# One 8 MB store ahead of the middle loads, issued as two halves on two queues (pairwise products of 32 fields)

## The chip, the core and the metric

The kernel runs on one core of a Trainium2 chip. The metric is device time in microseconds (us) of one execution, the median over runs. The engines that matter here are TensorE (PE), VectorE (DVE), and the two engines that only issue transfers in this kernel: SyncE (SP) and ScalarE (ACT). Each of the two has a queue of its own into the core's 16 DMA engines: in the profile SP's is q1 and ACT's is q10.

## The reference

For each of 4096 rows with 32 fields of 64 numbers, all fields are multiplied by one 64x64 matrix, and every pair of fields i < j gives one product, element by element. That makes 496 pairs, and an output of 4096 x 496 x 64 float32, 520 MB, from an input of 33.6 MB.

```python
vid = jnp.einsum('bfd,de->bfe', x, W)              # x: (4096, 32, 64), W: (64, 64)
idx_i, idx_j = jnp.triu_indices(32, k=1)           # 496 pairs
return x[:, idx_i, :] * vid[:, idx_j, :]           # (4096, 496, 64)
```

## The kernel before

**Tiles.** The batch is cut into 16 tiles (`NT`). A tile has 32 units, one for each field; a unit is 128 partitions x 128 float32 (two halves of the batch times 64 numbers on the partitions, 128 rows along a partition), 512 bytes on each partition. TensorE writes `vid` for one tile into PSUM in two halves of 16 fields. DVE multiplies: a unit of `x` in SBUF times a unit of `vid` gives a unit of the output, 496 of them to a tile.

**One buffer.** All of SBUF is one tensor, `mem`, of 445 units. The input lies in units 0 to 255, eight tiles at a time; `GROUPS` says so: group 0 is tiles 0 to 7, group 1 is tiles 8 to 15. The output is a stream of 7936 units, cut by the table `SLOTS` into 74 slots of 51 to 128 units. Each slot has a home in `mem`: as the input tiles of a group are used up, slots take their place. A slot is stored by one DMA when its last unit is made (`store`, L258). Slot 36, for example, is 128 units at home 304, so units 304 to 431, 8 MB in all, 64 KB to a partition.

**The middle loads.** When tile 8 begins (`t in begins[1:]`, L272), `load(1)` issues three loads for group 1: units 154 to 255 (6.7 MB, it holds tiles 8 and later), 26 to 153 (8.4 MB) and 0 to 25 (1.7 MB). Each waits (`after`, L201) until the stores that read its units have landed and DVE is done with the input there. In issue order the transfers are numbered `moved0`, `moved1` and so on; before the change `moved39`, `moved40` and `moved41` are the stores of slots 34, 35 and 36, and `moved42`, `moved43` and `moved44` are the three middle loads. The first store behind the loads, slot 37, also waits for the second of them (`hold[-2]`, L264).

**Queues.** Loads and the stores of slots 0 to 45 are issued by SP, in program order; those of slot 46 (`SECOND`) and later by ACT. An engine that issues stands still at an instruction until its semaphores are reached, so what stands behind it in its queue waits too. `Queue.waits` (L135) leaves out a wait that follows from an earlier one. `STRETCHES = [37]` marks slot 37 as the first slot behind the middle loads; so slot 36 is the last store ahead of them.

At the end SP waits for every transfer (L313).

Of the kernel before, what the change touches and what calls it, by code (L numbers as in the profile page):

```python
# [24 lines left out]
STRETCHES = [37]  # L25
# [17 lines left out]
SECOND = 46  # L43
# [128 lines left out]
def pairwise_bilinear_kernel(nc, x0, x, out):  # L172
# [8 lines left out]
    mem = ctx.enter_context(nc.sbuf_tensor([P, UNITS, C], F32))  # L181
# [8 lines left out]
    sp, act, dve = (Queue(engine, behind) for engine in (nc.sync, nc.scalar, nc.vector))  # L190
    moved = []
    worked = []

    def transfer(out_, in_, units, reads, needs, queue=sp):
        sem = nc.alloc_semaphore(f"moved{len(moved)}")
        queue.issue(lambda: queue.engine.dma_start(out=out_, in_=in_), needs).then_inc(sem, 16)  # L196
        queue.note(sem, 16)
        moved.append((units, reads, sem))
        return sem

    def after(units):  # L201

        needs = [(s, 16) for u, reads, s in moved if reads and overlap(u, units)]
        last = max((n for spans, n in worked if any(overlap(units, s) for s in spans)), default=0)
        return needs + [(made, last)] * (last > 0)
# [52 lines left out]
    def store(slot, last):  # L258
        nonlocal hold
        begin, end = STARTS[slot : slot + 2]  # L260
        home = SLOTS[slot][1]
        units = (home, home + end - begin)
        needs = [(made, last)]
        if hold:  # L264
            needs.append((hold[-2], 16))
            hold = []
        rows = out[BLOCKS[slot] : BLOCKS[slot + 1], :].rearrange("(p u) c -> p u c", p=P)
        transfer(rows[:, : end - begin, :], mem[:, units[0] : units[1], :], units, True, needs, act if slot >= SECOND else sp)


    for t in range(NT):
        if t in begins[1:]:  # L272
            hold = load(begins.index(t))
            for late in held:
                store(*late)
            held = []
        xs = (place_of(t, F), place_of(t, F) + F)
        blocks = list(products(by_block(), t * NP))
        for k, (at, n, nest, i, j) in enumerate(blocks):
            slot = bisect_right(STARTS, at) - 1  # L280
            begin, end = STARTS[slot], STARTS[slot + 1]
            home = SLOTS[slot][1]
            units = (home + at - begin, home + at - begin + n)
# [11 lines left out]
            needs = [(there, 2 * t + 2 - high), *after(units)]  # L295
# [9 lines left out]
            if at == end:  # L305
                late = (slot, counts[made])
                group = sum(behind <= slot for behind in STRETCHES)
                if t < begins[group]:
                    held.append(late)
                else:  # L310
                    store(*late)
# [65 lines left out]
```

## Time and profile before

| what | value |
|---|---|
| time, three runs | 1283.78, 1283.85, 1284.95 us; median 1283.85 us |
| span of the profiled execution | 1282.6 us (first to last instruction; what lies around it is no part of it) |
| bytes moved | 553.7 MB, 520.1 MB of them written to HBM |
| DVE busy | 1079.9 us, 84% of the span |
| PE busy | 179.4 us, 14% |
| last store before the middle loads (slot 36) | issued at 603.93 us, landed 38.0 us later |
| middle loads issued | from 622.22 us |

The page has the profiled execution's span alone; the median of the runs stands 1.25 us above it. Rows of a timeline begin with a time in us from the start of the span. In a table of stretches the last three columns are the granted TensorE clock, the share of time in which the 16 DMA engines were busy and the rate in GB/s. A packet is put down whole to the stretch in which it starts, so a short stretch can show a share over 1.

### The profile page before, as it was taken

Reading aid. Unit: us, or ns where it says so; the run is one execution under the profiler, and the core shown is the slowest. Engines: PE = TensorE matmul, PEld = TensorE weight load, DVE = VectorE, ACT = ScalarE, POOL = GpSimd, SP = SyncE. Lnnn points to the kernel's source line nnn. Section 1 sums busy time; section 2 is a strip of 40 time slices with the busy share of each in tenths; the row PEclk is TensorE's granted clock in tenths of the full one; section 3 lists DMA queues with packets and bytes.
Section 4 is the critical chain, followed back from the end, with each engine's and each line's share of the span. In section 5 each row is a group of like instructions: output and inputs, shape, how many; then the busy total and the mean of one; then the engine's idle time right before and its main releaser. Section 6 shows DMA issues by size and latency. Waiting matters only on the chain. (4 is left out here: it accounts for less than half of the span.)

```text
span 1282.6 us, 1255 instructions
## 1 busy us (share of the span) xinstructions
PE 179.4 (14%) x256; PEld 70.2 (5%) x256; DVE 1079.9 (84%) x273; POOL 0.2 (0%) x4
## 2 busy tenths in 40 slices
PE   2011120301111030300020111103020020201100
PEld 1000000100000010100010000001010010100000
DVE  6589989988897989998027989989988899899980
POOL 0000000000000000000000000000000000000000
PEclk8566565756656565655565655656556575656555
DMA  9999999999999999999999999999999999999999
GB/s 404 423 435 435 438 433 433 439 435 425 435 444 429 425 437 442 428 425 446 416 426 437 426 433 436 438 434 434 439 431 442 421 437 435 427 446 429 434 425 409
DMA packets 11810, 553.70 MB, mean 432 GB/s; under 512 B 1312, under 2 KB 1312, under 8 KB 1312
## 3 DMA queue, kind: packets, MB, share of 16 engines
q1 hardware_dynamic: 7776, 340.30, 61.5%
q10 hardware_dynamic: 4032, 213.39, 38.4%
q14 instruction: 2, 0.02, 0.0%
HBM read 33.59 MB, written 520.09 MB: 432 GB/s over the span
## 5 line engine op out<-in xcount | busy, mean ns | idle before, releaser
L299 DVE TENSOR_TENSOR mem<-mem,vid 128x1024 f32<-128x1024 f32 (+11 forms) x270 | 1079.3, 4065 | 161.2 <-DMA out_dram<-mem 114.5
L319 PE MATMUL vid<-mem,w 128*128 x256 | 179.4, 866 | 1016.1 <-PEq L317 1016.1
L319 PEld LDWEIGHTS vid<-mem,w 128*128 128x128 f32 x256 | 70.2, 288 | 1124.4 <-issue 1124.4
L230 DVE COPY w<-mem 64x64 f32<-64x64 f32 x2 | 0.4, 191 | 5.1 <-DMA mem<-in_r_x_dram 5.0
L227 DVE MEMSET w<- 128x128 f32 x1 | 0.2, 165 | 0.8 <-PEq L344 0.8
L344 POOL MEMSET const-bfloat16-1.0<- 128x1 bf16 x1 | 0.1, 101 | 0.0
L344 POOL MEMSET const-uint8-127<- 128x1 uint8 x1 | 0.1, 101 | 0.0
L344 POOL MEMSET const-float32-0.0<- 128x1 f32 x1 | 0.1, 98 | 0.2 <-issue 0.2
L344 POOL MEMSET const-float32-1.0<- 128x1 f32 x1 | 0.1, 98 | 0.0
## 6 DMA issues: line engine op xcount, KB each, us to landing
out_dram<-mem ACTq DMA_DIRECT2D x9, 7680.0 KB, 23.3
out_dram<-mem SPq DMA_DIRECT2D x4, 6656.0 KB, 20.5
out_dram<-mem SPq DMA_DIRECT2D x3, 7680.0 KB, 23.1
out_dram<-mem ACTq DMA_DIRECT2D x3, 7168.0 KB, 21.5
out_dram<-mem SPq DMA_DIRECT2D x5, 4096.0 KB, 17.5
out_dram<-mem SPq DMA_DIRECT2D x3, 5632.0 KB, 18.4
out_dram<-mem SPq DMA_DIRECT2D x3, 5120.0 KB, 17.3
out_dram<-mem SPq DMA_DIRECT2D x2, 7168.0 KB, 22.6
```

The source lines that it names most:

```text
L227: work(lambda: nc.vector.memset(w2[:, :], 0.0), [], [], made)
L230: lambda: nc.vector.tensor_copy(w2[half, half], mem[half, place + F, :D]),
L299: lambda: nc.vector.tensor_tensor(o, left, right, ALU.mult),
L319: last = nc.tensor.matmul(vid[:, b : b + BANK, :], lhsT=w2[:, :], rhs=xt(b), start=True, stop=True)
L344: nc = _bacc.Bacc("TRN2", target_bir_lowering=False, num_devices=1, dynamic_dma_scratch_size=512)
```

## The change

Slot 36 goes out in two halves of 64 units, 4.2 MB each. The first half (units 304 to 367) is issued by SP where the whole store stood. The second half (units 368 to 431) is issued by ACT, and waits for one thing more: the store before it (slot 35, `moved40`) must have landed. All other slots go as before.

```diff
         begin, end = STARTS[slot : slot + 2]
         home = SLOTS[slot][1]
-        units = (home, home + end - begin)
...
-        transfer(rows[:, : end - begin, :], mem[:, units[0] : units[1], :], units, True, needs, act if slot >= SECOND else sp)
+        parts = [(0, end - begin, needs, act if slot >= SECOND else sp)]
+        if slot + 1 in STRETCHES:
+            half = (end - begin) // 2
+            parts = [(0, half, needs, sp), (half, end - begin, [*needs, (moved[-1][2], 16)], act)]
+        for lo, hi, needs, queue in parts:
+            units = (home + lo, home + hi)
+            transfer(rows[:, lo:hi, :], mem[:, units[0] : units[1], :], units, True, needs, queue)
```

On SP, around the middle loads, before (-) and after (+); a row is one DMA, with the elements that it moves on each partition and the semaphores that it waits for, and 128x16384 is a slot of 128 units:

```order
-L196 DMA out_dram<-mem 128x16384 [waits made] x6
+L196 DMA out_dram<-mem 128x16384 [waits made] x5
+L196 DMA out_dram<-mem 128x8192 [waits made]
 L196 DMA mem<-in_r_x_dram 128x13056 [waits moved40,moved39]
 L196 DMA mem<-in_r_x_dram 128x16384
 L196 DMA mem<-in_r_x_dram 128x3328 [waits made]
-L196 DMA out_dram<-mem 128x13312 [waits moved43,made]
+L196 DMA out_dram<-mem 128x13312 [waits moved44,made]
```

The last of six large stores has become a half; the loads stand where they stood with the same waits, and behind them only the number of the second load has gone up by one.

On ACT, at the start of its program (it issues nothing but stores):

```order
-L196 DMA out_dram<-mem 128x10880 [waits barrier_Pool_Activation_PE_DVE_SP_release,made]
+L196 DMA out_dram<-mem 128x8192 [waits barrier_Pool_Activation_PE_DVE_SP_release,moved40,made]
+L196 DMA out_dram<-mem 128x10880 [waits made]
 L196 DMA out_dram<-mem 128x13696 [waits made]
 L196 DMA out_dram<-mem 128x14336 [waits made]
```

The second half now stands ahead of ACT's first store (slot 46), and waits for `moved40`, the same landing that SP's first middle load waits for.

On DVE, at the end of tile 7 and the first products of tile 8, in the kernel after:

```order
L304 TENSOR_TENSOR mem<-mem,vid 128x1024 [waits moved40]
L304 TENSOR_TENSOR mem<-mem,vid 128x8192 [waits moved41,there]
L304 TENSOR_TENSOR mem<-mem,vid 128x4096
L304 TENSOR_TENSOR mem<-mem,vid 128x2048 [waits moved42]
L304 TENSOR_TENSOR mem<-mem,vid 128x1024
```

The first product of tile 8 (128x8192) waits for the first half only (`moved41`), where it waited for the whole store; the third (128x2048), which had no wait, now waits for the second half (`moved42`).

## The prediction

> **What bounds the kernel now.** I read the page first, engine shares and then the transfers.
>
> ```profile
> PE 179.4 (14%) x256; PEld 70.2 (5%) x256; DVE 1079.9 (84%) x273; POOL 0.2 (0%) x4
> DMA  9999999999999999999999999999999999999999
> DMA packets 11810, 553.70 MB, mean 432 GB/s; under 512 B 1312, under 2 KB 1312, under 8 KB 1312
> ```
>
> DVE is busy for 84% and has 200 us to spare; the DMA engines are at nine tenths or more in every slice. To see whether they are at their peak I asked for the busy time in long stretches (the last three columns are TensorE's clock, the DMA engines' busy share, GB/s):
>
> ```profile
> core 0: us, PE busy (x) PEld busy (x) DVE busy (x) POOL busy (x), PEclk, DMA share, GB/s
> 60.00:560.00 500.00, 80.54 (x112) 31.29 (x112) 461.88 (x119) 0.00 (x0) 0.59 1.00 434
> 830.00:1270.00 440.00, 58.04 (x80) 22.57 (x80) 386.79 (x87) 0.00 (x0) 0.56 1.00 434
> ```
>
> Both long stretches stand at 434 GB/s with the engines fully busy. At that rate 553.70 MB take 553.70 / 0.434 = 1275.8 us, and the span is 1282.6. So the kernel's time is its bytes, and only 6.8 us lie outside: the start, the end, and the places where the transfers turn from one direction to the other. The change moves no byte more or less. It can give only what is lost at the middle loads, and cost only what it makes the DMA engines lose anew.
>
> Next, the place itself. SP's timeline and the DMA issues there (one row for an issue: KB, where they are known, and us to landing), and the first waits of DVE:
>
> ```profile
> 603.93 0.33 SPq L196 DMA_DIRECT2D out_dram<-mem  x1
> out_dram<-mem SPq DMA_DIRECT2D x1, 38.0
> 622.22 50.90 SPq L196 DMA_DIRECT2D mem<-in_r_x_dram  x3
> mem<-in_r_x_dram SPq DMA_DIRECT2D x1, 6528.0 KB, 35.9
> mem<-in_r_x_dram SPq DMA_DIRECT2D x1, 54.9
> 622.18 1.22 DVE L299 TENSOR_TENSOR mem<-mem,vid 128x1024 f32<-128x1024 f32 x1 [18.28 <-DMA out_dram<-mem]
> 664.08 8.69 DVE L299 TENSOR_TENSOR mem<-mem,vid 128x8192 f32<-128x8192 f32 x1 [40.68 <-PE vid L319]
> ```
>
> Slot 36's store is issued at 603.93 and lands at 641.9. The store before it lands at 622.2, which lets the loads out at 622.22; the first lands at 658.1, PE works on it, and DVE goes on at 664.08 after 40.68 us of standing still. That wait looks like the thing to shorten, but the DMA engines are full meanwhile, so it costs nothing by itself.
>
> What is lost there I read from short stretches, each cut so that it holds one round of packets, one on each of the 16 engines. Stretch times share is the mean time of a packet; stretch times rate, by 16, its size.
>
> ```profile
> 633.00:633.80 0.80, 0.00 (x0) 0.00 (x0) 0.00 (x0) 0.00 (x0) 0.50 3.03 1311
> 637.80:638.60 0.80, 0.00 (x0) 0.00 (x0) 0.00 (x0) 0.00 (x0) 0.50 3.92 1311
> 641.00:642.20 1.20, 0.00 (x0) 0.00 (x0) 0.00 (x0) 0.00 (x0) 0.50 1.80 696
> 643.10:644.40 1.30, 0.00 (x0) 0.00 (x0) 0.00 (x0) 0.00 (x0) 0.50 1.49 643
> 39.50:43.50 4.00, 0.00 (x0) 0.00 (x0) 0.77 (x2) 0.00 (x0) 0.50 1.15 422
> 675.50:682.00 6.50, 0.00 (x0) 0.00 (x0) 6.50 (x4) 0.00 (x0) 0.50 1.02 426
> 782.60:783.50 0.90, 0.00 (x0) 0.00 (x0) 0.90 (x1) 0.00 (x0) 0.50 1.35 583
> ```
>
> A 64 KB store packet takes 0.80 x 3.03 = 2.42 us; slot 36's last one takes 0.80 x 3.92 = 3.14, 0.71 more. The load's first packet takes 1.20 x 1.80 = 2.16 against 1.30 x 1.49 = 1.94 for the next, 0.22 more. The turn from store to load thus costs 0.71 + 0.22 = **0.93 us**, on all engines at once. The turn back, from load to store, is seen twice: 4 x (1.15 - 422/434) = 0.71 us near 41, and 6.5 x (1.02 - 426/434) = 0.25 us near 679.
>
> **The change part by part.**
>
> *Two halves for one.* Each engine moves eight packets of 64 KB for slot 36 before, sixteen of 32 KB after. A 32 KB packet is 0.90 x 1.35 = 1.215 us (last row above; 583 x 0.90 / 16 = 32.8 KB). Sixteen of them less eight of 2.42 make 19.44 - 19.36, about **+0.06 us**. The added issue on ACT, and the wait for one semaphore more at the very end, are nothing: ACT has had no work up to 785, and an issue is 0.33 us on an engine that isn't waited for.
>
> *When the second half comes.* It waits for slot 35's landing, so it goes out at 622.2, together with the first load. From an issue to its first packet about 1.0 us pass, by the kernel's start: the first load is issued at 0.73 and no packet starts before 1.70.
>
> ```profile
> 0.73 2.57 SPq L196 DMA_DIRECT2D mem<-in_r_x_dram  x5
> 0.00:1.70 1.70, 0.00 (x0) 0.00 (x0) 0.17 (x1) 0.20 (x4) 1.00 0.00 0
> ```
>
> So it can start at 623.2. Slot 36's first packet starts 7 x 2.42 = 16.9 us before the last one's 637.8, at 620.9; by 623.2 each engine has done about two of its eight packets of 32 KB. Six are left, 7 us of work: the engines don't run dry before the load and the second half are there. That is the cover for the shorter store in SP's queue, and it would have to be 7 us shorter to cost anything.
>
> *Who shares the engines then.* The first half's six packets and the loads stand in q1, the second half's eight in q10. If the engines take one packet from each queue in turn at once, six of the second half go between those of the first, and the last two beside the load's first ones. If the queue in progress is drained first, up to all eight stand beside the load. The trace of before has one place where both queues hold packets:
>
> ```profile
> 785.14 0.38 ACTq L196 DMA_DIRECT2D out_dram<-mem  x1
> DMA packets 50, 1.57 MB, mean 437 GB/s; under 512 B 3, under 2 KB 3, under 8 KB 3
> q1 hardware_dynamic: 47, 1.44, 92.7%
> q10 hardware_dynamic: 3, 0.13, 8.4%
> ```
>
> These are ACT's first store, and the queues from 785.2 to 788.8. In those 3.6 us, 2.6 more than an issue needs, 44 data packets still start on q1 and three on q10. So two to eight pairs of load and store are to be expected, nearer to eight. In every case the load's first packet now starts while a store from the other queue still has packets. The bytes ahead of the first load's landing are the same, so that landing, PE and DVE stay at 658 to 664 within a microsecond or two.
>
> *The turn.* Between two bounds: with the other queue's packets to fill it, the 0.93 us of the store-to-load turn are gone, and nothing comes in their place (-0.93). Or every change from a store's packet to a load's and back is paid: each further pair costs 0.93 + 0.25 to 0.71, so 1.2 to 1.6 us. No row shows a load and a store in turns. I take the lower bound, by this row-based reason: the turn shows as longer packets on a queue that goes on without a gap, so it reads as latency (the load's data aren't there when the store's are done), and latency is what work from another queue covers. The Trainium skill (DMA: Bandwidth & Descriptors, "Latency and other measured facts") gives 214 GB/s in each direction at full rate for copies on the two queues; by that, as an estimate, loads and stores in turns lose next to nothing, 428 GB/s in sum against the 434 measured here. That speaks for the lower bound too.
>
> *DVE's waits.* The first product of tile 8 needs only the first half, and starts at 664.08 by its wait for PE anyway: no gain. The third product has a new wait, for the second half. It starts at 664.08 + 8.69 + 4.33 (half a 128x8192 product) = 677 or so; the second half lands by about 650 even with eight pairs, 27 us earlier. If that cover were gone, everything on DVE would be late, and with it slot 38's store:
>
> ```profile
> 677.58 11.48 SPq L196 DMA_DIRECT2D out_dram<-mem  x2
> out_dram<-mem SPq DMA_DIRECT2D x1, 6656.0 KB, 20.4
> 672.79 0.33 SPq L196 DMA_DIRECT2D mem<-in_r_x_dram  x1
> ```
>
> Slot 37's store is out at 677.58 and lands at 698.0; slot 38's follows at about 688.7, so 8 us more are free there. The third load (issued at 672.79, after DVE's first product) keeps its place about 3 us ahead of the end of the second load's data (near 676), since both hang on the first load's landing.
>
> *Sum:* -0.93 + 0.06 = -0.87 us on the span, 1281.7. With the 1.25 us by which the median of the runs is above the span: 1283.85 - 0.87 = **1283.0 us**. That is 0.07%, under the 0.2% (2.6 us) that a measurement of this kernel can tell from no change.
>
> **The rivals.**
>
> 1. *The turn stays.* The second half only joins the queue of bytes, drained whole ahead of the load or as slow at the turn as before: +0.06, **1283.9 us**. For it: the 785 rows, where one queue drained before the other began. Against it: there the later store came alone, with no load behind the draining one. The Trainium skill (same page, "Issuing engines are not separate DMA queues") says that transfers from several engines share the same 16 DMA engines, and that only issue time is saved. By that rule the change would bring nothing, this rival's time; the rows agree on the shared rate (434 from q1 alone, 434 from q10 alone).
> 2. *Turns multiply (slower).* Loads and stores take turns packet by packet and each turn is paid. Two pairs cost 2 x 1.2 to 2 x 1.6, plus 0.06: 1286.3 to 1287.2. Eight pairs, with the turn that was there before taken off, 7 x 1.2 to 7 x 1.6: up to 11.6 us, **1292 to 1295**. It decides from two or three paid pairs on. For it: both directions of the turn have a price in the trace, 0.93 and 0.25 to 0.71. Against it: the price at 679 is a third of that at 41, so it isn't a fixed fee.
> 3. *Both directions at once go over 434.* If the engines moved a load and a store beside each other faster than either alone, the second half's eight packets would in part be free; at a third of its 9.7 us, 3.2 us are won: **1280.6**. For it: loads and stores never met in the trace, so no row forbids it. Against: an engine moves a load's packet at 52.2 KB / 1.94 us and a store's at 65.5 KB / 2.42 us, both 27 GB/s, so the limit looks like the engine's own, whatever the direction.
>
> **How the numbers follow.** Turn hidden, 0.48; turn stays, 0.30; turns multiply, 0.14; both directions faster, 0.05; something unlisted (the second half held up so long that DVE's third product waits past 685), 0.03. The predicted time is the first case's, 1283.0. The range runs from 1282.2 (the hidden turn, with the 0.8 us by which a median of a few runs may be off, the runs of before lie 1.17 us apart) to 1286.6 (two pairs paid): it leaves out the third rival and the longer part of the second. Faster by over 0.2% is the third rival and a little of noise: 0.06. Slower by over 0.2% is most of the second and the unlisted: 0.15. The rest, 0.79, is no change that can be told.
>
> **What would show it.** In the profile after: q10 has 4.2 MB more and its first packets near 623 to 631; the rate stays at 434 through 618 to 660; the round of packets ahead of the first load isn't 0.7 us longer. DVE's two waits (18.28 and 40.68) stay within 2 us of what they were. Right by steps: the third product of tile 8 has no wait in front of it. I am wrong if packets get longer between 623 and 660 by more than 2.5 us in sum, if slot 38's store is late and a stretch behind 690 falls below 430, or if the loads' landing moves by more than 3 us with the end.

## The result and the profile after

| | median, us | runs |
|---|---|---|
| before | 1284.30 (1283.78 to 1285.99) | 21 |
| after | 1286.17 (1285.73 to 1287.44) | 21 |

The ratio is 1.0015, with a 95% interval of 1.0008 to 1.0021: the change costs 1.87 us. The span of the profiled execution went from 1282.6 to 1285.2 us; the time of the execution after is 1286.55.

The page of the kernel after, its two queues (number, packets, MB, share):

```profile
q1 hardware_dynamic: 7776, 336.10, 60.7%
q10 hardware_dynamic: 4176, 217.58, 39.2%
```

4.2 MB have gone over to ACT's queue, as meant. Next the middle loads. The timeline after, in order: the loads' issue on SP and the second half's on ACT, DVE's restart with tile 8, SP's third load by itself, and DVE's restart when slot 37's store has landed:

```profile
622.22 53.58 SPq L196 DMA_DIRECT2D mem<-in_r_x_dram  x3
622.24 0.38 ACTq L196 DMA_DIRECT2D out_dram<-mem  x1
666.76 8.69 DVE L304 TENSOR_TENSOR mem<-mem,vid 128x8192 f32<-128x8192 f32 x1 [43.36 <-PE vid L324]
675.48 0.33 SPq L196 DMA_DIRECT2D mem<-in_r_x_dram  x1
700.61 4.88 DVE L304 TENSOR_TENSOR mem<-mem,vid 128x384 f32<-128x384 f32 x2 [6.98 <-DMA out_dram<-mem]
```

The DMA issues of the same kernel near 622, with KB and us to landing: the first load and the second half.

```profile
mem<-in_r_x_dram SPq DMA_DIRECT2D x1, 6528.0 KB, 38.2
out_dram<-mem ACTq DMA_DIRECT2D x1, 4096.0 KB, 29.5
```

The second half goes out at 622.24 beside the first load, as forecast, and lands at 651.7. But the first load lands 38.2 us after its issue, not 35.9. DVE goes on at 666.76, not 664.08, the third load is out at 675.48, not 672.79, and slot 37's store lands at 700.6. The same row of before, 2.6 us earlier:

```profile
697.98 13.48 DVE L299 TENSOR_TENSOR mem<-mem,vid 128x384 f32<-128x384 f32 x3 [7.04 <-DMA out_dram<-mem]
```

That is as much as the difference between the two spans. The landing of slot 35 is at 622.2 in both, so the time goes between 622 and 700.

The rates there, a stretch before:

```profile
634.00:644.00 10.00, 0.00 (x0) 0.00 (x0) 0.00 (x0) 0.00 (x0) 0.50 0.92 356
```

and three after:

```profile
634.00:644.00 10.00, 0.00 (x0) 0.00 (x0) 0.00 (x0) 0.00 (x0) 0.50 1.03 345
646.00:660.00 14.00, 0.00 (x0) 0.00 (x0) 0.00 (x0) 0.00 (x0) 0.50 1.02 442
660.00:674.00 14.00, 9.04 (x16) 3.75 (x16) 7.24 (x1) 0.00 (x0) 0.82 1.00 435
```

Share and rate count the same packets, so length x (share - rate / 434) is how much longer they took than their bytes need at 434 GB/s, whatever the edges cut; it is good to about 0.1 us and leaves out time in which an engine had nothing to do. I call it the loss. At the turn from store to load it is 10 x (0.92 - 356/434) = **1.00 us** before and 10 x (1.03 - 345/434) = **2.35 us** after. The queues after the change, from 634 to 644 (packets, MB, share), say which packets got longer:

```profile
q10 hardware_dynamic: 56, 1.84, 53.2%
q1 hardware_dynamic: 48, 1.61, 49.4%
```

q10 is the store. Its packets took 10 x 0.532 - 1.84/0.434 = 1.1 us too long (mean over the engines), where the last store packets before the change took 0.71. q1 is nearly all load there, and its packets took 10 x 0.494 - 1.61/0.434 = 1.2 us too long, where the load's first packets took 0.22. So most of the added cost sits in the load's own first packets.

From 646 to 660 the loss is 14 x (1.02 - 442/434) = 0.0. Yet both queues still had packets there:

```profile
DMA packets 151, 6.18 MB, mean 442 GB/s; under 512 B 31, under 2 KB 31, under 8 KB 31
q1 hardware_dynamic: 119, 5.66, 93.3%
q10 hardware_dynamic: 32, 0.52, 8.7%
```

0.52 MB of q10 are sixteen 32 KB packets, one on each engine, beside 5.66 MB of q1's load. So a load and a store in turns cost a lot at their first meeting and nothing a few packets later. That split of the cost is what the experiments are about.

### The profile page after: what moved, and what is told of

It reads as the page before. It is cut to its first block, busy times and chain, and to the rows that moved or that the text cites. A ratio compares the mean times of both kernels' runs of the same rounds, so it can differ in the third digit from the quotient of the medians.

```text
span 1285.2 us, 1257 instructions
## 1 busy us (share of the span) xinstructions
PE 186.5 (15%) x256; PEld 72.2 (6%) x256; DVE 1079.9 (84%) x273; POOL 0.2 (0%) x4
## 5 line engine op out<-in xcount | busy, mean ns | idle before, releaser
L324 PE MATMUL vid<-mem,w 128*128 x256 | 186.5, 897 | 1011.8 <-PEq L322 1011.8
```

The costliest lines, as they stand in the source:

```text
L324: last = nc.tensor.matmul(vid[:, b : b + BANK, :], lhsT=w2[:, :], rhs=xt(b), start=True, stop=True)
```

## The experiments

All times are beside runs of the kernel before on the same chip: 1284.24 for the first four; 1284.34 for the second half without its wait, the late half and `SECOND = 37`; 1284.27 for the small part on ACT and the repeats; 1284.59 for the seam.

**Both halves on SP.** Is it the second queue, or the smaller packet in front of the load?

```diff
-            parts = [(0, half, needs, sp), (half, end - begin, [*needs, (moved[-1][2], 16)], act)]
+            parts = [(0, half, needs, sp), (half, end - begin, needs, sp)]
```

> Slot 36 still goes out in two halves of 32 KB packets, but both from SP, one after the other, so no store shares the engines with the loads and ACT starts with slot 46 as before the change. Theory A (the two queues are the cost: packets of a store and of a load taken in turns pay for each change): the loss at the turn from store to load, 1.0 us before and 2.35 us after the change, is back at 1.0; time +0.1 us on the kernel before (ratio 1.0000 to 1.0003). Theory B (packet size is the cost: the engines begin a load's read only one packet ahead, so the packet in front of the load covers its latency, 2.42 us when it has 64 KB and 1.21 us when it has 32 KB): the loss stays at 2.2 to 2.4; time +1.3 to +1.9 us (ratio 1.0010 to 1.0015).

**A small tail on SP**, 112 and 16 units, by `half = end - begin - 16` with the same `parts`:

> Slot 36 is cut into 112 and 16 units, both from SP: the last packets ahead of the load are 8 KB (0.31 us each, eight on each engine, 2.5 us in all). Theory A: no second queue, so a loss of 1.0 us at the turn, and +0.1 to 0.2 us for small packets. Theory B with a read-ahead of just one packet: only 0.3 us of cover, a loss of about 3.2 us, time +2.2 us on before. Theory B with a read-ahead counted in bytes, or in many packets: a loss near 1.0 here, and then the size of a packet is not what counts.

The turn with two halves on SP:

```profile
634.00:644.00 10.00, 0.00 (x0) 0.00 (x0) 0.00 (x0) 0.00 (x0) 0.50 1.05 408
```

and with the small tail:

```profile
634.00:644.00 10.00, 0.00 (x0) 0.00 (x0) 0.00 (x0) 0.00 (x0) 0.50 1.02 390
```

Two halves on SP lose 10 x (1.05 - 408/434) = 1.1 us and take 1284.21 us, ratio 0.9999 (0.9990 to 1.0008). The tail loses 1.2 and takes 1284.85, ratio 1.0005 (0.9996 to 1.0014). Theory B falls: a packet an eighth as large in front of the load costs 0.1 to 0.2 us more, not 2. Splitting alone costs nothing that the time shows. What is left is the second queue.

**The loads on ACT.** Slot 36 whole on SP, in 64 KB packets, the middle loads on the other queue:

```diff
-            sems.append(transfer(mem[:, lo:hi, :], x[:, at : at + hi - lo, :], (lo, hi), False, after((lo, hi))))
+            sems.append(transfer(mem[:, lo:hi, :], x[:, at : at + hi - lo, :], (lo, hi), False, after((lo, hi)), act if g else sp))
```

> Slot 36 is whole again, from SP in 64 KB packets; the three middle loads go out from ACT instead. The first load is issued at 622.2 on the other queue and up to six or seven of slot 36's packets stand beside it. Theory A: many changes between a store's packet and a load's, each paid: a loss of 3 us and more between 620 and 660, time +2 to +6 us on before. Theory B: the first load's read is covered by a 64 KB packet, the loss is 1.0 us or less and time is within 0.3 us of before; if the loss vanishes (-0.9 us), a second queue does hide the turn when the packets are large.

The stretch of the first meeting and the one after it:

```profile
622.00:636.00 14.00, 0.00 (x0) 0.00 (x0) 1.18 (x1) 0.00 (x0) 0.50 0.97 363
636.00:650.00 14.00, 0.00 (x0) 0.00 (x0) 0.00 (x0) 0.00 (x0) 0.50 1.02 441
```

and the queues' packets and MB in the second of them:

```profile
q1 hardware_dynamic: 52, 3.41, 56.1%
q10 hardware_dynamic: 53, 2.77, 45.6%
```

It takes 1285.22 us, ratio 1.0010 (1.0001 to 1.0019). The loss is 14 x (0.97 - 363/434) = 1.9 us up to 636, and 14 x (1.02 - 441/434) = 0.1 from 636 to 650, with 52 packets of slot 36's store among 53 of the load. So theory A holds in one half: the second queue makes the turn dearer. It falls in the other: three or more pairs on each engine in a row are free. And a large packet doesn't make the second queue hide the turn. The loss doesn't go into the time one for one: the profiled run with these 1.9 us took 1284.25 us, and two profiled runs of the kernel before, told of below, took 1284.09 and 1283.98. The turn back is cheaper there, 10 x (1.00 - 428/434) = 0.1 us from 674 to 684 against 0.3 before.

**Halves by partitions**, 64 partitions each, so that packets keep 64 KB:

```diff
+            parts = [(0, P // 2, needs, sp), (P // 2, P, [*needs, (moved[-1][2], 16)], act)]
+        for lo, hi, needs, queue in parts:
+            transfer(rows[lo:hi, : end - begin, :], mem[lo:hi, units[0] : units[1], :], units, True, needs, queue)
```

> As after the change, a first half from SP and a second from ACT behind slot 35's landing, but cut by partitions (0 to 63, 64 to 127), so each packet keeps its 64 KB. Theory A: as after the change, +1.3 to +1.9 us. Theory B: the loss at the turn falls back to about 1.0 us, time within 0.4 us of before. A third way: each half may use the engines unevenly, since its rows lie on half of the partitions; then packets are longer than 2.42 us already ahead of the loads.

```profile
622.00:630.00 8.00, 0.00 (x0) 0.00 (x0) 1.22 (x1) 0.00 (x0) 0.50 0.65 131
630.00:660.00 30.00, 0.00 (x0) 0.00 (x0) 0.00 (x0) 0.00 (x0) 0.50 0.99 319
```

1300.55 us, ratio 1.0128 (1.0112 to 1.0143). The first row holds one packet of each engine (8 x 131 / 16 = 65.5 KB), so its share says how long that packet took: 8 x 0.65 = 5.2 us, where 2.42 is usual. (Its 131 GB/s is no rate, since a packet is put down whole where it starts.) Packets are that long before a load moves, so this is the third way, and the run says nothing on A or B. Why a store from half of the partitions is that slow wasn't tried further.

**The second half without its wait.** It goes out near 604, and is gone before the loads come:

```diff
-            parts = [(0, half, needs, sp), (half, end - begin, [*needs, (moved[-1][2], 16)], act)]
+            parts = [(0, half, needs, sp), (half, end - begin, needs, act)]
```

> As after the change, two halves on SP and ACT, but the second half no longer waits for slot 35's landing: it goes out as soon as it is made, near 604, runs beside slot 35 and is gone before the loads come; only the first half, in 32 KB packets, stands ahead of the first load, all in SP's queue. Theory A2 (a load that meets a store from the other queue makes the one turn from store to load dearer, once, and pairs after that are free): no meeting, so the loss at the turn is that of two halves on SP, 1.1 to 1.3 us, and time within 0.4 us of before. Theory A3 (splitting a store over the two queues costs by itself, loads or not): the loss is spread over the stretch in which slot 35 and the second half run together, 606 to 632, and time is 1 us or more above before.

**The second half late.** It waits for the first load's landing (`hold[0]`) and so meets the second load, with loads running (`rest` holds that half):

```diff
+            for out_, in_, units, needs in rest:
+                transfer(out_, in_, units, True, [*needs, (hold[0], 16)], act)
```

> The first half goes out from SP, the second from ACT only when the first middle load has landed, so that it meets the second load, with loads running. The first turn has one queue and 32 KB packets: a loss of 1.1 to 1.3 us near 632. Theory A2 in its strict form (only a load's first arrival among stores is paid; a store that joins running loads is free): no loss from 650 to 680, time within 0.4 us of before. Theory A4 (the first turn each way is paid, store to load 1.1 and load to store 0.7 or more, and only then is the mixture free): 0.7 to 1.3 us more near 652, time +0.7 to +1.5 us. DVE's third product of tile 8 waits for the half until about 680; slot 38's store has 3 us or more to spare by then.

Without the wait: the stretch in which slot 35 and the second half run together, and the turn.

```profile
606.00:632.00 26.00, 0.00 (x0) 0.00 (x0) 1.22 (x1) 0.00 (x0) 0.50 0.99 429
634.00:644.00 10.00, 0.00 (x0) 0.00 (x0) 0.00 (x0) 0.00 (x0) 0.50 1.03 403
```

The late half: its two turns (one queue, then the store that joins) and the stretch behind them.

```profile
624.00:634.00 10.00, 0.00 (x0) 0.00 (x0) 0.00 (x0) 0.00 (x0) 0.50 1.03 397
646.00:658.00 12.00, 8.33 (x15) 3.62 (x16) 2.44 (x1) 0.00 (x0) 0.66 0.98 400
658.00:674.00 16.00, 0.96 (x3) 0.13 (x1) 10.58 (x2) 0.00 (x0) 0.70 1.02 440
```

Without the wait: 26 x (0.99 - 429/434) = 0.0 us with two stores side by side, 10 x (1.03 - 403/434) = 1.0 at the turn, 1284.21 us, ratio 0.9999 (0.9990 to 1.0008). So ACT's queue costs nothing by itself: where the second half doesn't meet the load, the dearer turn and the longer time are both gone. The late half loses 10 x (1.03 - 397/434) = 1.2 us at the first turn, 12 x (0.98 - 400/434) = 0.7 where the store joins the running loads, and 0.1 from 658 to 674 in mixture. It takes 1284.90 us, ratio 1.0005 (0.9996 to 1.0014). The loss where the store joins is the least that theory A4 allowed (0.7 to 1.3); the time, 0.56 us above before, lies between A2's 0.4 and A4's 0.7 and decides nothing.

**A small part on ACT**, 112 and 16 units with the wait as after the change:

> As after the change (second part on ACT, behind slot 35's landing), but cut into 112 and 16 units: the part on ACT has 8 KB packets, 1 MB in all, and two or three of the eight on each engine should be left when the load's first packets come. Theory A4 (what is paid is the first change each way between queues, whatever the size of what stands beside the load): a loss of 2.0 to 2.5 us from 634 to 650, time +0.9 to +1.5 us on before. Theory A5 (the price goes with the bytes that stand beside the load): a loss of 1.2 to 1.6, time within 0.6 us of before.

```profile
634.00:644.00 10.00, 0.00 (x0) 0.00 (x0) 0.00 (x0) 0.00 (x0) 0.50 1.01 374
644.00:654.00 10.00, 0.00 (x0) 0.00 (x0) 0.00 (x0) 0.00 (x0) 0.50 0.99 429
```

1.5 us at the turn, 0.0 behind it, 1284.51 us, ratio 1.0003 (0.9994 to 1.0012). A4's fixed price is too high here and A5's fits: little stands beside the load, and little is paid. But A5 has no room for loads_act, where larger packets lost 1.9 and not more than 2.35. So the price is paid once, lies between 0.4 and 1.35 us above the single queue's turn, and no rule for its size came out.

**Stores on ACT from slot 37 on** (`SECOND = 37`), so that the turn back crosses queues:

> Slot 36 whole on SP as before; the stores from slot 37 on go out from ACT, not from slot 46 on, so the turn from the last load to the first store near 680 crosses queues. With the three loads on ACT that turn cost nothing, against 0.2 to 0.3 us with one queue. If crossing hides it, time is 0.2 us under before, which can be seen in the profile's stretch alone; if crossing makes a turn dearer whatever its direction, the stretch from 675 to 690 loses 1 us or more.

1284.38 us, ratio 1.0002 (0.9993 to 1.0012), and from 674 to 684 a loss of 10 x (0.95 - 394/434) = 0.4 against 10 x (0.95 - 399/434) = 0.3 before: nothing gained.

```profile
674.00:684.00 10.00, 0.00 (x0) 0.00 (x0) 10.00 (x4) 0.00 (x0) 0.50 0.95 394
```

The same stretch before:

```profile
674.00:684.00 10.00, 0.00 (x0) 0.00 (x0) 10.00 (x4) 0.00 (x0) 0.50 0.95 399
```

**The changed kernel and the kernel before, again.** The dearer turn is 1.1 to 1.35 us of 1.87.

> The changed kernel once more, for a second profile: the loss at the turn is to be 2.2 to 2.6 us between 634 and 646, and nothing from 650 to 674, if the one profile is typical.

> The changed kernel again, on the same chip as the experiments, since the first comparison (+1.87 us) is more than the 1.1 to 1.4 us that its profiles lose at the middle loads. If the rest belongs to the change, the time is again +1.6 to +2.1 us on before and the profile shows a loss elsewhere than from 634 to 650; if it is chance of one chip or time, the time is +0.9 to +1.5 us.

> The kernel before, as a control: a ratio of 1.0000 within 0.0003, a loss of 1.0 to 1.4 us at the turn from store to load, and 0.2 to 0.4 us at the turn back near 680.

> The changed kernel, one more look: the loss from 674 to 692 grows with the time at which the third load is issued (0.02 at 674.6, 0.49 at 675.5, 1.25 at 676.4).

> The changed kernel, the last look: again the loss from 674 to 692 should follow the time at which the third load goes out, and the loss near 640 be 2.0 to 2.5 us.

The changed kernel's median in these rounds was 1285.94 us, ratio 1.0011 (1.0002 to 1.0020); the control's ratio was 1.0001 (0.9992 to 1.0010). Its five profiles have the loss at the turn (634 to 644) at 2.35, 2.15, 1.96, 2.17 and 2.16; three of the kernel before, one with the seam that is told of below, at 1.00, 1.01 and 1.11. The difference is 1.1 us in the mean, and at least 0.85. The rest of the cost isn't in every profiled run:

| profiled run | third load issued, us | slot 37 landed (DVE restarts), us | time, us |
|---|---|---|---|
| after_again | 674.60 | 699.05 | 1285.07 |
| after_5 | 674.92 | 699.04 | 1285.62 |
| after | 675.48 | 700.61 | 1286.55 |
| after_4 | 675.83 | 700.58 | 1286.52 |
| after_third | 676.37 | 700.81 | 1287.04 |

The landing moves by a step: up to 674.9 slot 37 lands at 699.05, 1.0 us later than before; from 675.5 on, at 700.6 to 700.8, which is 1.6 us more. The mean loss from 674 to 684 grows in the same order, 0.1, 0.1, 0.4, 0.7 and 0.9 us. The third load comes too late there to follow the second without a gap: its first packet starts 0.1, 0.3 and 0.5 us after the first engine has ended the second load in the traces of after, after_4 and after_third, and at once in the other two.

**An earlier third load.** It waits for DVE's first product of tile 8; a seam in `SLOTS`, which divides a product of DVE, makes it 8 and 56 units, so the load can go out after the first 8. The same seam in the kernel before is the control.

```diff
-    (128, 176), (128, 304), (128, 32), (128, 160), (128, 304), (104, 256), (85, 360),
+    (128, 176), (128, 304), (128, 32), (128, 160), (128, 304), (104, 256, 16), (85, 360),
```

> The changed kernel, with the first product of tile 8 cut into 8 and 56 units. The third middle load waits for that first product to end, so it goes out about 7.6 us earlier, near 667 to 669 instead of 674.6 to 676.4, well ahead of the end of the second load. If its lateness is the rest of what the change costs, the loss from 674 to 692 is at most 0.3 us and the time is 0.3 to 0.8 us under the changed kernel's, +0.9 to +1.3 us on before. If not, time stays at +1.6 to +1.9 us. The loss at the turn near 640 is 2.1 to 2.5 us in both cases.

> The kernel before with the same cut, one product more on DVE: its third load had 3 us to spare already, so the time is that of before, within 0.3 us, and the loss at the turn from store to load 1.0 to 1.4 us.

> The changed kernel with the earlier third load, a second look. A typical run (near 1285.8) should lose 1.3 us more than the look before. If the turn near 640 varies, it is found there (3 us and more); if the rest of the run varies, it is found from 692 on (1 us and more); the stretch from 674 to 692 stays under 0.3 us.

> The same kernel as in the look before, a third look, for the same split of its time: the turn near 640, the turn back near 680, and the rest.

The third load and slot 37's landing, in the first profile of the changed kernel with the seam:

```profile
667.07 0.33 SPq L196 DMA_DIRECT2D mem<-in_r_x_dram  x1
698.38 13.48 DVE L304 TENSOR_TENSOR mem<-mem,vid 128x384 f32<-128x384 f32 x3 [5.62 <-DMA out_dram<-mem]
```

and in the control:

```profile
666.06 0.33 SPq L196 DMA_DIRECT2D mem<-in_r_x_dram  x1
698.04 13.48 DVE L299 TENSOR_TENSOR mem<-mem,vid 128x384 f32<-128x384 f32 x3 [6.30 <-DMA out_dram<-mem]
```

With the seam, the third load is out at 667.0 to 667.8, and slot 37 lands at 698.38, 698.63 and 698.70 in the three profiled runs: the step is gone, so the late third load was its cause, and 0.3 to 0.7 us above the control are left. The turn still loses 1.90, 2.15 and 1.90, under the 2.1 to 2.5 that I expected in two of three. It loses 0.8 to 1.0 more than in the control, but the turn back from 674 to 684 wins some back: 0.1 us is lost there, 10 x (1.01 - 435/434) in the first run, against 10 x (0.94 - 397/434) = 0.25 in the control.

The time is too coarse to confirm it: a median of 1285.76, ratio 1.0009 (1.0000 to 1.0018), where the control had 1284.31, ratio 0.9997 (0.9988 to 1.0006). I expected 0.9 to 1.3 us above before, and 1285.76 - 1284.59 = 1.2 is inside. The changed kernel without the seam was 1285.94 - 1284.27 = 1.7 above its own runs of before, so the gain is 0.5 us, and each of the two figures is only good to about 1 us.

From slot 37's landing to the end of the run, the control took 1283.98 - 698.04 = 585.9 us, the first profiled run 1284.40 - 698.38 = 586.0, and the other two 587.0 and 587.1 (1285.66 and 1285.83). So about 1 us is lost after 700 in two of the three profiled runs. The queue from 1281 on, in the first run and in the second:

```profile
q10 hardware_dynamic: 16, 0.00, 0.3%
q10 hardware_dynamic: 17, 0.06, 4.3%
```

Sixteen tiny packets end the last store. In the second run, and in the third too, one engine also starts a large packet that late, and it ends about 1 us behind the other fifteen (at 1283.85, when they were done by 1282.84; in the third run 1284.02 and 1283.20). In the first run the last two ended together, at 1282.7. So most of this loss is one engine that ends late. Why it is late, and whether the change makes it so, is open.

## Why the prediction was wrong, step by step

The time, 1286.17, lies in the stated range (1282.2 to 1286.6), but the forecast was a gain of 0.87 us, and it was a loss of 1.87. That it lies in the range is no credit to the forecast's own case: the range reaches that far only because it was drawn up to the second rival's two paid pairs.

- *What bounds the kernel, and how much can be lost there:* right. The stretches from 646 to 674 stand at 434 GB/s and over, and what changed is how long the engines lose time between 622 and 700.
- *Two halves for one, +0.06 us; the cover of 7 us:* right within the measurement. Two halves on SP run at a ratio of 0.9999. (19.44 - 19.36 is 0.08, not 0.06; nothing hangs on it.)
- *When the second half comes:* right. It was issued at 622.24, and about three of its eight packets on each engine stood beside the load, between the two and eight that the step gave.
- *The turn:* this is the step that failed. Between -0.93 and a price for every pair I took the lower bound, for the reason that a longer packet on a queue without gaps "reads as latency", which "work from another queue covers". The runs showed the opposite sign: with the other queue's stores there, the turn costs 2.2 us and not 1.0, and with 64 KB packets, 1.9. Nothing was covered: the store's packets ahead of the load were still too long, and the load's first packets lost 1.2 us where they had lost 0.22. The upper bound was wrong as well: no pair after the first few costs anything. Neither bound held because both took all pairs to be alike. The Trainium skill's 214 GB/s in each direction for copies between HBM tensors (DMA: Bandwidth & Descriptors, "Latency and other measured facts"), 428 in sum as an estimate, is near what the mixture does once it runs (441 GB/s from 636 to 650 with the loads on ACT). It says nothing of the first meeting, which is where the time went.
- *The first load's landing stays, and the third load keeps its 3 us:* wrong as well. The first load's landing came 2.3 us later, which is more than the 1.35 us that the engines lost in the mean: a landing waits for the slowest engine. The third load is issued behind that landing, but its place in the queue comes up when the engines are done with the second load, and the first of them was only 0.9 us later (676.0 and 676.85). So of the 3.2 us from the third load's issue to its first packet (672.79 to 676.0) 1.5 were left (675.48 to 677.0), and in three profiled runs of five that was too little.
- *DVE's waits:* right for the third product, which had no wait in front of it, and for the 18.28 us, which stayed at 18.18. The other wait grew from 40.68 to 43.36 us, by 2.68, where it was to stay within 2.
- *The signs of being wrong:* too wide. Packets between 623 and 660 were to get longer by more than 2.5 us in sum and the landing to move by more than 3; they got 1.35 us longer than before, and it moved by 2.3. The sign that did show was the rate: it was to stay at 434, and from 634 to 644 it was 345, less than the 356 of before.
- *The rivals:* the second ("turns multiply") came nearest. Two paid pairs were to cost 2.4 us, and 1.87 was measured. That its 1286.3 is within 0.2 us of the measured time is in part luck: the sum starts from 1283.85, and the kernel before stood at 1284.30 beside the change. Nor is its mechanism what happened: three pairs on each engine, from 636 to 650 with the loads on ACT, were to cost 3.6 us and more, and lost 0.1. (It also counts in two ways: for eight pairs the old turn is taken off, for two it isn't.) The first rival, with the Trainium skill's rule on shared engines (DMA: Bandwidth & Descriptors, "Issuing engines are not separate DMA queues"), would have been nearer than my forecast: where only stores share the engines, ACT's queue changes nothing (1284.21 without the wait), as the rule says. Where a store meets a load it does, by 1.1 us; there the measurement decides.

The sum as it turned out: +1.1 for the dearer turn, and 1.6 for the late third load in three of five profiled runs, 1.0 in the mean: 2.1 against the measured 1.87. It is a rough sum, since the first term is a mean over the engines and the second a landing. Why one engine ends late in two of the runs with the seam is not explained, and the first of the two terms is shown as a fact and not as a mechanism: why the engines lose more when the first load's neighbours come from another queue stays open.

No version of the change beats the kernel before. The best, with two halves and no meeting of queues, are at ratios of 0.9999.

## What to carry to other kernels

With the DMA engines full, the second queue was no cover here: putting a store beside the first load made the turn dearer by 1.1 us, and the same split cost nothing in one queue or where only stores met. Price the first meeting of two streams apart from their steady mixture, since a rate measured in steady state says nothing of it. And take a margin from the slowest engine, not from the mean: of 3.2 us that seemed safe only 1.5 were left when one transfer in front landed 2.3 us late, and that was too little.

## What the runs showed of the hardware

- One turn from store to load in one queue costs about 1.0 us in the mean over the 16 engines, with packets of 64, 32 or 8 KB in front of it (1.0, 1.1, 1.2).
- Where a store from the other queue is still there, the turn costs 2.0 to 2.35 us (five profiles); in the kernel after, 1.2 us of it in the load's first packets, against 0.22 before.
- Loads and stores in turns from two queues run at the full rate after their first packets: a loss of 0.1 us in 14 with 52 and 53 packets of the two kinds.
- A packet from the second queue started only about 4 us after its issue: from 622.3 to 626.0, q1 alone had packets, in the profile of the kernel after.

```profile
DMA packets 48, 1.57 MB, mean 425 GB/s; under 512 B 0, under 2 KB 0, under 8 KB 0
q1 hardware_dynamic: 48, 1.57, 99.5%
```

- A 64 KB packet of a store from 64 partitions took 5.2 us, against 2.42 us in a store from 128 partitions.
